# Graph network, third layer: messages written in place, scores made ahead from broadcast keys, block ends spread out, three edge counts to a word

## The chip, the cores and the metric

The kernel runs on one core of a Trainium2 chip. The metric is the device time of one execution in microseconds (us), the median of several runs. Its engines are TensorE (PE in the profile; PEld is its weight load), VectorE (DVE), ScalarE (ACT), GpSimd (POOL) and SyncE (SP). Each works through its own list of instructions in order. SP issues plain transfers, POOL the indirect ones that gather rows by index; both are carried out by 16 DMA engines.

## The reference

Four graph layers work in turn on 6250 nodes of 256 features and 100000 edges sorted by target; each adds its result to `x` and normalises. The change is in the third, two graph-attention passes, and in a table that the fourth uses:

```python
# third layer, one pass (two are made, each followed by gelu); edges and one self loop per node
h = (h_in @ W).reshape(n, 4, 64)
alpha_s = jnp.sum(h * a_s, axis=-1); alpha_d = jnp.sum(h * a_d, axis=-1)
e = leaky_relu(alpha_s[src] + alpha_d[dst], 0.2)
ex = exp(e - m[dst])                       # m: maximum over a target's edges
alpha = ex / segment_sum(ex, dst)[dst]
out = segment_sum(h[src] * alpha[:, :, None], dst) + b
# fourth layer
msg_sum = segment_sum(x[src], dst); mean = msg_sum / max(count, 1)
sage = mean @ W_l.T + b_l + x @ W_r.T
out = relu(relu(sage) @ W_ln.T + x)
```

## The kernel before

The nodes are cut into 50 blocks of 125. The edges that lead to a block lie in 16 chunks of 128 (and two chunks of overflow that 25 blocks share). A piece is four chunks of one block, so a pass over the edges makes 200 pieces. For each pass the table `hs_table` in device memory holds a row of 264 numbers per node: 256 features, four source scores and four target scores.

`piece2` handles one piece. It gathers the 4 x 128 source rows into a tile `g` (four indirect transfers on POOL, one per chunk; `gather`, L932) and makes one-hot matrices `st` from the target keys (DVE, `one_hots`, L941). To give each edge its target's score, PE transposes the one-hots (L2085), ACT copies them as bf16 into `ts` (L2088), and PE multiplies them with the block's target scores, kept as three bf16 parts `ad_parts` (L2093, twelve products into `pe`). DVE adds source and target scores (`e`, L2049) and applies the leaky relu (`r`, L2043); ACT takes exponentials twice, into a small strip of PSUM (`weights_p`, which shares a PSUM tile with the constant `iota_p` and goes by that name in the profile, L2052) and into the last column of the message tile (L2053). DVE multiplies features and weights into the message tile `msg` (L2055). PE sums the messages by target with the one-hots into `ps` (L2127; f32 products appear twice each). Self loops enter through a tile `own`, loaded by SP, its messages `mine`, and a product with the identity (L2120). After a block's last piece, `finish2` divides by the summed weights, adds the bias, takes gelu (L2002 to L2011), and either makes the next pass's table row (first pass) or normalises `x` and writes two tables for the fourth layer (second pass).

The order on PE, DVE and ACT is written out by hand. A piece is a generator that yields group names. `Turns` calls, once a turn, the groups in a fixed order; a plain name means "in the next turn", a "+" in front "later in this turn". A turn starts one new piece, so about six pieces are under way: new, transposes, copy and score products, `e`, product, sum. The order on POOL and SP follows the order in which their instructions are made. POOL is ahead of the others as far as free `g` tiles (nine) allow.

Beside the pieces, in most turns, `count_edges` makes one step of another job: for the first 24 blocks of targets it counts the edges from each source to each target, into `a_table` (bytes). For a source block and a range of four target blocks (500 columns), DVE makes one-hots `a_hot` per chunk (L1965), PE sums them by source (L1975), ACT writes bytes and checks the sum (L1951). There are six ranges, in which 3, 5, 4, 7, 8 and 6 chunks can hold edges: 33 per source block.

Of the kernel before, what the change touches and what calls it, by code (L numbers as in the profile page):

```python
# [17 lines left out]
P = 128  # L18
# [638 lines left out]
def gnn_stack_kernel(ctx: ExitStack, tc: tile.TileContext, ins, out):  # L657
# [55 lines left out]
    ND, RB = 24, 4  # L713
    RW, NR = RB * B, ND // RB
    assert ND % (2 * RB) == 0 and ND < NB and RW <= 512 and NB % 2 == 0
    reach = []
    for r in range(NR):
        e0, e1 = (E * k * RW / N for k in (r, r + 1))
        g0, g1 = (
            int((e + side * 5.5 * (e * (1 - e / E)) ** 0.5) // (GQ * EQ)) for e, side in ((e0, -1), (e1, 1))  # L720
        )
        c0 = max(0, int(place_of(g0 * GQ * EQ, -1)) // P) if g0 else 0
        reach.append((c0, min(CM, int(place_of((g1 + 1) * GQ * EQ, 1)) // P + 1)))
    DC = max(c1 for c0, c1 in reach)
    COUNT_STEPS = NB * NR
# [16 lines left out]
    with ExitStack() as fast:  # L742
# [8 lines left out]
        nc.gpsimd.iota(pidx, pattern=[[1, 1]], base=0, channel_multiplier=1, allow_small_or_imprecise_dtypes=True)  # L751
        ident = const.tile([P, P], F32, name="ident")
# [37 lines left out]
        xr_table = dram.tile([N, D], F32, name="xr_table_f")  # L790

# [210 lines left out]
        def by_target(pool, psum):  # L1002
# [76 lines left out]
            yield  # L1079
            p_row = psum.tile([1, NB + 1], F32, name="p_row")  # L1080
# [504 lines left out]
        class Turns:  # L1585
# [7 lines left out]
            def step(self, item):  # L1593
                group = next(item[0], None)
                if group is None:
                    self.items.remove(item)
                elif group[0] == "+":
                    item[1:] = group[1:], self.now
                else:
                    item[1:] = group, self.now + 1  # L1600
# [8 lines left out]
        def run_pass(turns, makers, beside=None):  # L1609

            for t, make in enumerate(makers):
                turns.add(make())
                turns.turn()
                if t >= len(makers) - 10:
                    turns.turn()
                if beside:
                    beside(t)
# [141 lines left out]
        def features(work, bank, a, w, b, table):  # L1759
# [11 lines left out]
            yield "+fin"  # L1771
            ad, r = hs[:, D + 4 :], work.tile([B, 4], F32, name="ad_r")
# [158 lines left out]

        def count_edges():


            nodes = ap.tile([P, RB, B], F16, name="a_nodes", bufs=1)
            nc.vector.scalar_tensor_tensor(
                nodes, iota[:, :RB, None].to_broadcast([P, RB, B]), float(B),
                iota_p[:, None, :B].to_broadcast([P, RB, B]), op0=ALU.mult, op1=ALU.add,
            )
            nodes = nodes.rearrange("p b n -> p (b n)")  # L1940
            ends = ap.tile([P, NB, DC], F32, name="a_ends", bufs=1)
            nc.vector.tensor_copy(ends, idx_s[:, :, :DC])
            most = max(c1 - c0 for c0, c1 in reach)
            steps = [(s, r) for s in range(NB) for r in range(NR)]
            sts, rows, accs, hots = {}, {}, {}, {}
            for k in range(len(steps) + 2):
                if k >= 2:
                    s, r = steps[k - 2]
                    if r == 0:
                        rows[s] = ap.tile([B, ND * B], U8, name="a_row")  # L1950
                    nc.scalar.activation(  # L1951
                        rows[s][:, r * RW : (r + 1) * RW], accs.pop((s, r))[:B], AF.Copy,
                        accum_out=counted[:B, s * NR + r : s * NR + r + 1],
                    )
                    if r == NR - 1:
                        move(nc.sync, a_table[s * B : (s + 1) * B, :], rows.pop(s))
                        del sts[s]
                if k < len(steps):
                    s, r = steps[k]
                    c0, c1 = reach[r]  # L1960
                    if s not in sts:
                        sts[s] = one_hots(ap, key_s[:, s, :DC], DC, DC, 2, F16, "a_st")
                    hots[k] = ap.tile([P, most, RW], F16, name="a_hot", bufs=2)
                    for i, c in enumerate(range(c0, c1)):
                        nc.vector.tensor_scalar(  # L1965
                            hots[k][:, i, :], nodes, ends[:, s, c : c + 1], float(-r * RW), op0=ALU.subtract,
                            op1=ALU.is_equal,
                        )
                if 0 <= k - 1 < len(steps):
                    s, r = steps[k - 1]  # L1970
                    c0, c1 = reach[r]
                    hot = hots.pop(k - 1)
                    accs[s, r] = apsum.tile([P, 512], F32, name="a_acc")[:, :RW]
                    for i, c in enumerate(range(c0, c1)):
                        nc.tensor.matmul(  # L1975
                            accs[s, r], sts[s][:, c, :], hot[:, i, :], start=(c == c0), stop=(c == c1 - 1)
                        )
                yield

        counted = ap.tile([P, NB * NR], F32, name="counted", bufs=1)  # L1980
        nc.vector.memset(counted, 0.0)
        counting = count_edges()


        for layer in range(2):
            table = hs_tables[layer]
            with tc.tile_pool(name=f"f2{layer}", bufs=1) as pool, tc.tile_pool(
                name=f"f2w{layer}", bufs=2
            ) as work, tc.tile_pool(name=f"f2g{layer}", bufs=9) as gp, tc.tile_pool(
# [6 lines left out]
                turns = Turns(("act", "e", "msg", "fin", "ps", "late", "pe", "tp", "new"))  # L1996

                def finish2(b):
                    whole = sums.pop(b)
                    ps = whole[:B, : D + H2].rearrange("p (h c) -> p h c", h=H2)  # L2000
                    rden = rdens[:B, b, 4 * layer : 4 * layer + 4, None]
                    nc.vector.tensor_scalar(rden, ps[:, :, C2:], 1e-30, None, op0=ALU.max)  # L2002
# [3 lines left out]
                        a.rearrange("p (h c) -> p h c", h=H2), ps[:, :, :C2], rden.to_broadcast([B, H2, C2])  # L2006
                    )
                    nc.vector.tensor_add(a, a, bias[:B, :])
                    yield "act"
                    gl = work.tile([B, D], F32, name="gl")  # L2010
                    nc.scalar.activation(gl, a, AF.Gelu)  # L2011
                    if layer == 0:
                        yield "+late"
                        yield from features(work, lambda: whole, gl, w_gat, b, hs_tables[1])
                    else:
                        yield "+fin"
                        nc.vector.tensor_add(x_sb[:, b, :], x_sb[:, b, :], gl)
                        norm(work, b, False)
                        yield "act"
                        xp = work.tile([B, 3, D], BF16, name="xp")  # L2020
                        nc.scalar.copy(xp[:, 0, :], x_sb[:, b, :])
                        yield "+fin"
                        x_r = work.tile([B, D], F32, name="x_r")
                        nc.vector.tensor_sub(x_r, x_sb[:, b, :], xp[:, 0, :])
                        yield "+late"
                        pt = turned(whole, x_sb[:, b, :])
                        yield "act"
                        nc.scalar.copy(xp[:, 1, :], x_r)
                        xT = kept(work, pt, "xT")
                        yield "+fin"  # L2030
                        nc.vector.tensor_sub(xp[:, 2, :], x_r, xp[:, 1, :])
                        move(nc.sync, block_rows(x_table, b), xp.rearrange("p k d -> p (k d)"))
                        yield "+late"
                        product(whole[:B, :D], [(xT, w_r)])
                        yield "act"
# [4 lines left out]
                def weights(e, n, parts):  # L2040

                    r = work.tile([P, 4, H2], F32, name=f"r{parts}")[:parts, :n, :]
                    nc.vector.scalar_tensor_tensor(r, e, 0.2, e, op0=ALU.mult, op1=ALU.max)  # L2043
                    return r.rearrange("p n h -> p (n h)")

                def messages(g, n, ad, msg, k):

                    e = work.tile([P, 4, H2], F32, name="e")
                    nc.vector.tensor_add(e[:, :n, :], g[:, :n, D : D + 4], ad)  # L2049
                    r = weights(e[:, :n, :], n, P)  # L2050
                    pp = weights_p[:, 4 * H2 * k : 4 * H2 * (k + 1)]
                    nc.scalar.activation(pp[:, : n * H2], r, AF.Exp)  # L2052
                    nc.scalar.activation(msg[:, : n * H2, C2], r, AF.Exp)  # L2053
                    yield "msg"
                    nc.vector.tensor_mul(  # L2055
                        msg[:, : n * H2, :C2].rearrange("p (n h) c -> p n h c", h=H2),
                        g[:, :n, :D].rearrange("p n (h c) -> p n h c", h=H2),
# [304 lines left out]
```

## Time and profile before

| what | value |
|---|---|
| median of 3 runs (lowest, highest) | 5450.11 us (5446.99, 5450.46) |
| the profiled execution | 6347.38 us |
| its span, first to last instruction | 6345.5 us |
| mean granted clock of PE in it | 0.876 |
| first pass of the third layer, first to last L2055 | 2844.3 to 4133.4 us |
| second pass | 4197.4 to 5560.4 us |
| gathers of the two passes (L932, hs_table) | 1600, mean 951 ns |

The profile shows a single execution, which is longer than the runs without it. Busy times can't be added across engines, since they overlap. A row of waits reads: engine and line that waited, "<-" what released it, total us, times, longest. In a row of a group, the part after "|" gives busy us and the mean ns of one instruction, then the idle time of the engine before it.

### The profile page before, as it was taken

What the parts mean: (1) busy time and instruction counts of PE and PEld (TensorE: products, weight loads), DVE (VectorE), ACT (ScalarE), POOL (GpSimd) and SP (SyncE); (2) the same over time, 40 slices, a digit from 0 to 9 for tenths busy, and PEclk for the clock granted to TensorE, in tenths of its full rate; (3) what the DMA queues carried; (4) which work ended last, traced back from release to release, by engine and by line L of the source; (5) the groups of instructions that cost most, each with busy time, mean ns of one, the idle gap of its engine ahead of it and who ended that gap; (6) DMA issues with size and microseconds to landing.
All of it is one profiled execution on the core that took longest, in us unless ns stands there. A gap on an engine that the chain in (4) does not pass through costs nothing.

```text
span 6345.5 us, 85961 instructions
## 1 busy us (share of the span) xinstructions
PE 4651.2 (73%) x28778; PEld 3328.7 (52%) x28778; DVE 3995.7 (63%) x11239; ACT 2312.8 (36%) x6308; POOL 3590.8 (57%) x3709
## 2 busy tenths in 40 slices
PE   1567888867777777757777777747766776779996
PEld 0445666645555555535555555535545555545554
DVE  7786666646777777746666666646767767623233
ACT  4016677932322222213333333323333333323332
POOL 5776666645555555535555555455555555455554
PEclk9778999988999999978888888878888878889997
DMA  5555555545655556533333333333333333377774
GB/s 152 152 163 157 160 157 151 153 129 170 177 173 171 172 167 174 171 86 96 105 102 102 102 101 101 90 83 102 104 100 104 105 102 97 93 189 206 205 193 122
DMA packets 383758, 862.39 MB, mean 136 GB/s; under 512 B 85018, under 2 KB 208376, under 8 KB 383304
## 3 DMA queue, kind: packets, MB, share of 16 engines
q0 software_dynamic: 221184, 670.83, 39.0%
q1 hardware_dynamic: 162120, 185.97, 10.2%
q8 instruction: 228, 3.74, 0.2%
q14 instruction: 226, 1.85, 0.1%
HBM read 769.69 MB, written 86.78 MB: 135 GB/s over the span
## 4 chain that ended last, share of the span: by engine, by line
PE 35%; DVE 22%; issue 13%; another core or an unknown queue 10%; ACT 9%; POOL 5%; DMA 3%; SPq 0%; DVEq 0%; ACTq 0%; POOLq 0%
PE ps L2127 6%; PE d L2274 6%; POOL g L932 5%; PE ps L985 5%; PE a_acc L1975 4%; DVE msg L2055 3%; PE po L928 2%; DVE s L1821 2%; PE tp L2085 2%; DVE msg L1828 2%; PE acc L1519 2%; DVE a_hot L1965 2%; DMA g<-kv_table_f,idx_s 2%; PE pt L928 2%
## 5 line engine op out<-in xcount | busy, mean ns | idle before, releaser
L932 POOL DMA_INDIRECT g<-hs_table_f,idx_d x1600 | 1520.9, 951 | 1249.8 <-DVE msg L2055 493.8
L932 POOL DMA_INDIRECT g<-kv_table_f,idx_s x784 | 746.7, 952 | 548.9 <-issue 204.2
L932 POOL DMA_INDIRECT g<-h_table_f,idx_d x800 | 799.5, 999 | 430.6 <-issue 213.8
L2127 PE MATMUL ps<-msg,st 128*125 128x260 f32 x3200 | 919.6, 434 | 97.2 <-DVE msg L2055 52.9
L2127 PEld LDWEIGHTS ps<-msg,st 128*125 128x125 f32 x3200 | 688.5, 218 | 291.6 <-issue 82.8
L1975 PE MATMUL a_acc<-a_hot,a_st 128*128 128x500 f16 x1650 | 497.6, 444 | 373.6 <-ACT a_row L1951 282.8
L2055 DVE TENSOR_TENSOR msg<-g,iota_p 128x1024 f32<-128x1024 f32 x400 | 488.2, 1221 | 403.6 <-ACT iota_p L2052 328.0
L932 POOL DMA_INDIRECT g<-x_table_f,idx_d x416 | 395.7, 951 | 383.4 <-PE ps L985 191.4
L985 PE MATMUL ps<-g,st 128*128 128x256 bf16 (+1 forms) x3648 | 519.3, 293 | 126.1 <-issue 60.4
L985 PEld LDWEIGHTS <-st 128*128 128x128 bf16 x4104 | 419.2, 104 | 255.8 <-issue 150.3
L2088 ACT CAST ts<-tp 125x512 bf16<-125x512 f32 x400 | 233.3, 583 | 820.7 <-remote 479.2
L1965 DVE TENSOR_SCALAR a_hot<-a_nodes,a_ends 128x500 f16<-128x500 f16 x1650 | 505.2, 372 | 18.1 <-remote 18.1
L1908 PE MATMUL ps<-msg,st 128*125 128x264 f32 x1600 | 437.7, 419 | 100.6 <-DVE msg L1828 73.3
L1975 PEld LDWEIGHTS <-a_st 128*128 128x128 f16 x1650 | 180.5, 109 | 577.1 <-issue 484.6
L1908 PEld LDWEIGHTS ps<-msg,st 128*125 128x125 f32 x1600 | 301.4, 199 | 237.3 <-DVE msg L1828 103.9
L941 DVE TENSOR_TENSOR st<-iota_p,key_d 128x500 f32<-128x500 f32 (+1 forms) x550 | 409.8, 746 | 20.8 <-ACT iota_p L2052 16.3
L2274 PE MATMUL d<-cnt,xs 125*128 125x500 bf16 x1800 | 401.2, 378 | 16.9 <-issue 16.5
L1889 DVE TENSOR_TENSOR prod<-g,qe 128x512 f32<-128x512 f32 x400 | 262.3, 684 | 197.5 <-PE qe L1882 68.3
L2049 DVE TENSOR_TENSOR e<-g,pe 128x16 f32<-128x16 f32 x400 | 65.1, 163 | 454.7 <-remote 352.1
L1882 PE MATMUL qe<-q,ts 125*128 125x256 bf16 x2400 | 318.9, 286 | 29.0 <-DVE prod L1889 24.2
L2085 PE MATMUL tp<-ident,st 128*125 128x128 f32 x1600 | 308.5, 314 | 40.6 <-issue 30.1
L1532 ACT ACTIVATE oa<-t_f,blk 125x128 f16<-125x128 f16 x800 | 310.7, 388 | 74.4 <-remote 48.1
(453 smaller groups left out, 8768.0 us busy)
## 6 DMA issues: line engine op xcount, KB each, us to landing
g<-hs_table_f,idx_d POOLq DMA_INDIRECT x1600
xs<-x_table_f SPq DMA_DIRECT2D x75, 336.0 KB
a_table_f<-a_row SPq DMA_DIRECT2D x50, 328.1 KB
few<-a_table_f SPq DMA_DIRECT2D x75, 218.8 KB
g<-h_table_f,idx_d POOLq DMA_INDIRECT x800
g<-kv_table_f,idx_s POOLq DMA_INDIRECT x784
hs_table_f<-hs SPq DMA_DIRECT2D x100, 115.5 KB
own<-hs_table_f SPq DMA_DIRECT2D x100, 115.5 KB
```

What stands on the lines that cost most here:

```text
L932: nc.gpsimd.indirect_dma_start(out=g, out_offset=None, in_=table, in_offset=bass.IndirectOffsetOnAxis(ap=idx, axis=0))
L941: nc.vector.tensor_tensor(st, iota_p[:, None, :w].to_broadcast([P, n, w]), key[:, :, None].to_broadcast([P, n, w]), op=ALU.is_equal,)
L985: nc.tensor.matmul(ps[:, :m], st[:, i, :], g[:, i, k * D : k * D + m], start=(c0 + i == 0 and k == 2), stop=(c0 + i == CH - 1 and k == 0),)
L1532: nc.scalar.activation(oa[:, i, :], o1[:, i, :], AF.Copy, scale=val_a[:, at])
L1882: nc.tensor.matmul(qe[:, i, :], ts[:, i0 + i, :], q[:, k * D : (k + 1) * D], start=(k == 0), stop=(k == 2))
L1908: nc.tensor.matmul(sums[b][:B, : D + H1], hot, m[:, i * H1 : (i + 1) * H1, :].rearrange("p h c -> p (h c)"), start=(c == 0), stop=(c == CH ...
L1965: nc.vector.tensor_scalar(hots[k][:, i, :], nodes, ends[:, s, c : c + 1], float(-r * RW), op0=ALU.subtract, op1=ALU.is_equal,)
L1975: nc.tensor.matmul(accs[s, r], sts[s][:, c, :], hot[:, i, :], start=(c == c0), stop=(c == c1 - 1))
L2055: nc.vector.tensor_mul(msg[:, : n * H2, :C2].rearrange("p (n h) c -> p n h c", h=H2), g[:, :n, :D].rearrange("p n (h c) -> p n h c", h=H2) ...
L2085: nc.tensor.transpose(tp[:, i, :], st[:, i, :], ident)
L2127: nc.tensor.matmul(sums[b][:B, : D + H2], hot, m[:, i * H2 : (i + 1) * H2, :].rearrange("p h c -> p (h c)"), start=False, stop=(c == CH - 1),)
L2274: nc.tensor.matmul(accs[h][q], xs[:, i, j * D + h * P : j * D + (h + 1) * P], cnt[:, i, q * RW : (q + 1) * RW], start=(s + i == 0 and j == 2),
```

## The change

1. *Scores from broadcast keys.* At the start, the keys of every block (an edge's place among the block's nodes) are written to device memory as bf16 rows (`keys_d`). `keys2` loads a block's row into all 125 partitions, so partition p can compare all 2048 keys with p: ACT computes (key - p) squared and then relu(1 - that), in place, four chunks at a time (`node_hots`). That gives the transposed one-hots of a whole block; PE multiplies them with `ad_parts` and ACT copies the 16 x 4 scores to `ends_d`. A pass starts with eight turns of keys alone (`LEAD_K`), and keys are begun eight turns ahead of their block's first piece. The per-piece transposes, `ts` and the per-piece `pe` go.
2. *In place.* The weights go into columns 256 to 259 of `g` (over the source scores), and the product into its feature columns; `own` is treated in the same way. PE sums from `g`. There is no `msg` or `mine` tile. `g` has 11 tiles instead of 9. The one-hots for the sum are made in the turn of the product.
3. *Block ends.* `Turns` takes a number ahead of a name ("3act": three turns later). A block's end moves from PE to ACT or DVE with one to three turns between. Four PSUM banks for sums instead of three; the groups have another order.
4. *Counts.* Three ranges of 500 columns share one accumulation: an edge adds 1, 256 or 65536 to the column, by its range. `less` and `unit` are made once for all chunks. Each source block has two such words, of 5 and 9 possible chunks, in steps of at most three: 14 instead of 33. ACT copies a word to int32 and then writes its low three bytes as three rows of counts.

The core of the diff:

```diff
+        keys_d = dram.tile([NB, CAP], BF16, name="keys_d_f")
...
+            k_rows = pool.tile([NB, CAP], BF16, name="k_rows")
+            nc.scalar.copy(k_rows, k_f)
+            nc.sync.dma_start(out=keys_d, in_=k_rows)
...
-                    item[1:] = group, self.now + 1
+                    name = group.lstrip("0123456789")
+                    item[1:] = name, self.now + int(group[: len(group) - len(name)] or 1)
...
+        LEAD_K = 8
+        def run_pass(turns, makers, beside=None, keys=None):
+            per = len(makers) // NB
+            for t in range(-LEAD_K if keys else 0, 0):
+                if (t + LEAD_K) % per == 0:
+                    turns.add(keys((t + LEAD_K) // per))
+                turns.turn()
             for t, make in enumerate(makers):
+                if keys and (t + LEAD_K) % per == 0 and (t + LEAD_K) // per < NB:
+                    turns.add(keys((t + LEAD_K) // per))
...
-                    hots[k] = ap.tile([P, most, RW], F16, name="a_hot", bufs=2)
-                    for i, c in enumerate(range(c0, c1)):
+                    hots[k] = ap.tile([P, 3, RW], BF16, name="a_hot", bufs=4)
+                    for i in reversed(range(n)):
                         nc.vector.tensor_scalar(
-                            hots[k][:, i, :], nodes, ends[:, s, c : c + 1], float(-r * RW), op0=ALU.subtract,
-                            op1=ALU.is_equal,
+                            hots[k][:, i, :], column, less[:, s, c0 + i : c0 + i + 1],
+                            unit[w][:, s, c0 + i : c0 + i + 1], op0=ALU.is_equal, op1=ALU.mult,
                         )
...
+                    word = ap.tile([B, RW], I32, name="a_word")
+                    nc.scalar.copy(word, accs.pop((s, w))[:B])
                     nc.scalar.activation(
-                        rows[s][:, r * RW : (r + 1) * RW], accs.pop((s, r))[:B], AF.Copy,
+                        rows[s][:, w * WORD * RW : (w + 1) * WORD * RW].rearrange("p (q j) -> p q j", q=WORD),
+                        word.bitcast(U8).rearrange("p (j q) -> p q j", q=4)[:, :WORD, :], AF.Copy,
...
+        G_BUFS, ST_BUFS = 11, 9
+        def node_hots(kb, q):
+            part = kb[:, q * 4 * P : (q + 1) * 4 * P]
+            nc.scalar.activation(part, part, AF.Square, bias=minus[:B])
+            nc.scalar.activation(part, part, AF.Relu, bias=ones[:B, 0:1], scale=-1.0)
...
-                turns = Turns(("act", "e", "msg", "fin", "ps", "late", "pe", "tp", "new"))
+                turns = Turns(("late", "keys", "pe", "keys2", "pe2", "e", "msg", "ps", "fin", "new", "act"))
...
+                def steps_of(g, n, ad, k, p=P):
+                    e = work.tile([P, 4, H2], F32, name="e")[:p, :n, :]
+                    nc.vector.tensor_add(e, g[:, :n, D : D + 4], ad)
+                    r = work.tile([P, 4, H2], F32, name="r")[:p, :n, :]
+                    nc.vector.scalar_tensor_tensor(r, e, 0.2, e, op0=ALU.mult, op1=ALU.max)
+                    pp = weights_p[:p, 4 * H2 * k : 4 * H2 * k + n * H2].rearrange("p (n h) -> p n h", h=H2)
+                    nc.scalar.activation(pp, r, AF.Exp)
+                    nc.scalar.activation(g[:, :n, D : D + H2], r, AF.Exp)
+                    yield "msg"
+                    feats = g[:, :n, :D].rearrange("p n (h c) -> p n h c", h=H2)
+                    nc.vector.tensor_mul(feats, feats, pp[:, :, :, None].to_broadcast([p, n, H2, C2]))
...
+                def keys2(b):
+                    kb = work.tile([B, CAP], BF16, name="kb")
+                    move(nc.sync, kb, keys_d[b : b + 1, :].to_broadcast([B, CAP]))
+                    yield "2keys"
+                    ts = kb.rearrange("p (c e) -> p c e", e=P)
+                    pe = psum.tile([P, CM, H2], F32, name="pe")
+                    for q in range(CM // 4):
+                        node_hots(kb, q)
+                        yield "+pe2" if q % 2 else "+pe"
+                        for c in range(4 * q, 4 * q + 4):
+                            for k in range(3):
+                                nc.tensor.matmul(
+                                    pe[:, c, :], ts[:, c, :], ad_parts[:, b, k, :], start=(k == 0), stop=(k == 2)
+                                )
+                        if q % 2:
+                            yield "keys"
+                        else:
+                            yield "+keys2"
+                    yield "act"
+                    ends_d[b] = work.tile([P, CM, H2], F32, name="ends_d", bufs=3)
+                    nc.scalar.copy(ends_d[b], pe)
...
-                    yield "tp"
-                    tp = psum.tile([B, 4, P], F32, name="tp", bufs=2)
-                    for i in range(n):
-                        nc.tensor.transpose(tp[:, i, :], st[:, i, :], ident)
-                    yield "act"
-                    ts = work.tile([B, 4, P], BF16, name="ts", bufs=3)
-                    nc.scalar.copy(ts[:, :n, :], tp[:, :n, :])
-                    yield "pe"
...
+                    yield "2e"
+                    steps = steps_of(g, n, ends_d[b][:, c0 : c0 + n, :], (c0 // 4) % 2)
...
+                    st = one_hots(work, key_d[:, b, c0 : c0 + n], n, 4, ST_BUFS)
...
-                        yield "fin"
+                        yield "3fin"
                         yield from finish2(b)
```

## The prediction

> **What bounds the kernel now.** I read the page's busy shares first, then one row per stage of the third layer, then who waits for whom in it. Each of the layer's two passes makes 200 turns of one piece (50 blocks of four pieces), and each turn has one wide message product on VectorE (L2055), so the pass is measured from the first of these to the last.
>
> ```profile
> span 6345.5 us, 85961 instructions
> PE 4651.2 (73%) x28778; PEld 3328.7 (52%) x28778; DVE 3995.7 (63%) x11239; ACT 2312.8 (36%) x6308; POOL 3590.8 (57%) x3709
> ```
> ```profile
> core 0: us, PE busy (x) PEld busy (x) DVE busy (x) ACT busy (x) POOL busy (x), PEclk, DMA share, GB/s
> 2844.00:4133.00 1289.00, 1001.43 (x6207) 722.84 (x6208) 839.23 (x2294) 439.99 (x1214) 730.65 (x770) 0.86 0.37 99
> 4197.00:5560.00 1363.00, 952.16 (x6052) 700.67 (x6052) 935.11 (x2670) 490.37 (x1306) 730.42 (x768) 0.83 0.36 99
> ```
>
> No engine is full. Per turn the first pass takes 1289/200 = 6.45 us and the second 6.82. Of this PE is busy 5.0 and 4.8, DVE 4.2 and 4.7, ACT 2.2 and 2.5. GpSimd shows 3.65 us, but one gather is 0.95 us and the next starts 0.30 later even with nothing to wait for:
>
> ```profile
> 4381.49 0.95 POOL L932 DMA_INDIRECT g<-hs_table_f,idx_d  x1 [0.30 <-issue]
> 4382.75 0.95 POOL L932 DMA_INDIRECT g<-hs_table_f,idx_d  x1 [0.30 <-issue]
> ```
>
> So four gathers need 4 x 1.25 = 5.0 us: the floor of a turn. What lies above it is waiting in a ring, as the waits of the second pass (GpSimd, VectorE) and of the first (ScalarE) show:
>
> ```profile
> POOL g L932 <- DVE msg L2055: 279.9, 106, 8.6
> POOL g L932 <- DVE rdens L2002: 104.2, 31, 4.6
> ...
> DVE e L2049 <- remote: 151.6, 41, 9.0
> DVE msg L2055 <- ACT iota_p L2052: 150.5, 126, 4.2
> DVE e L2049 <- PE pe L2093: 35.7, 28, 3.1
> ...
> ACT ts L2088 <- remote: 260.1, 45, 13.0
> ACT ts L2088 <- PE pe L2093: 103.5, 21, 7.5
> ACT ts L2088 <- PE tp L2085: 69.5, 32, 8.2
> ```
>
> GpSimd waits for the product that frees a gather tile; VectorE waits at the score sum `e` for PE; ScalarE waits at the copy `ts` for PE's transposes. "Remote" is a release without a recorded releaser: there the semaphore that `e` and `ts` wait for is PE's. The ring is one-hots (DVE), transposes (PE), `ts` (ACT), `pe` (PE), `e` (DVE), exponentials (ACT), product (DVE).
>
> **The base of the sum.** The profiled execution took 6347.38 us (span 6345.5), the runs 5450.11: 0.859 of it. I assume that ratio for the passes: 5.53 and 5.86 us a turn in the timed runs. I do not scale the 1.25 us of a gather, since nothing around it waits; that choice is the largest uncertainty here.
>
> **The change part by part.**
>
> *Scores from broadcast keys.* Out go, per turn, four transposes and one `ts` copy (0.586 us of ACT, L2088). The PE rows at full clock, start to start:
>
> ```profile
> 4373.87 0.45 PE L2093 MATMUL pe<-ad_parts,ts 125*128 125x4 bf16 x12
> 4374.18 0.68 PE L2085 MATMUL tp<-ident,st 128*125 128x128 f32 x4
> 4374.69 1.86 PE L1975 MATMUL a_acc<-a_hot,a_st 128*128 128x500 f16 x8
> 4376.39 0.60 PE L2120 MATMUL ps<-mine,ident 125*125 125x260 f32 x2
> ```
>
> Transposes take 0.51 us a turn, the 12 `pe` products 0.31 (they stay, 24 at a time in two of four turns), one count product 1.70/8 = 0.21. In come per block: eight ACT operations on 125x512 bf16 (nearest row L2088; its source is PSUM in f32, ends 0.45 to 0.65; I take 0.57) = 4.6 us against 4 x 0.586 = 2.3 before, a 128x64 copy (about 0.2) and one more exponential of the block's own rows (0.2): ACT +2.7 a block, 0.7 a turn, so 3.2 of 5.0. A key load of 2 x 125 x 2048 = 512 KB a block joins SP's queue: 99 GB/s at a share of 0.37 is about 268 GB/s in all, so 1.9 us on free engines, 3 on these; it is issued two turns (10 us) before use. On SP it stands behind the write of `xp`, which waits for VectorE; that write belongs to a block whose turn came earlier, so it delays keys by less than those two turns. What this buys: `e` now waits only for its gather and for scores copied five turns before. The PE waits at `e` (151.6 + 35.7) and all waits at `ts` go; where they go is GpSimd, which becomes the engine behind which everything stands.
>
> *In place.* The product writes into `g`: the same 1024 f32 elements, 1.22 us, no change. The tile is now held until PE has summed it, turn 4 after the gather, instead of the product in turn 5; 11 tiles instead of 9. The next gather can start 7 turns (35 us) ahead, against 4 before. So GpSimd should wait for none of the tiles.
>
> *Block ends three turns a hop.* The same instructions, about 5 us of DVE a block. In the steady part nothing waits for them: a sum's bank is held 15 turns of 16 (four banks). Two more blocks are unfinished when a pass ends: 2 x 5 = 10 us a pass, hidden by nothing. At its start eight turns hold keys alone: 16 x 0.57 = 9 us of ACT beside the first gathers (5 us, plus the table's last write), so I add 8. Both passes: 36.
>
> *Counts.* Products and `a_hot` fall from 33 to 14 a source block, 1650 to 700. PE saves 950 x 0.21 = 200 us, 0.5 a turn. An `a_hot` now takes two scalars from memory. The rows for that are the norm's (two pointers, 273 ns) and its first step (constants, 154):
>
> ```profile
> L1965 DVE TENSOR_SCALAR a_hot<-a_nodes,a_ends x1650: 329/341/590, 2802.1 to 5505.9; 128x500 f16<-128x500 f16 x184
> L864 DVE TENSOR_SCALAR ln_t<-ln_y,ln_w x300: 272/273/275, 1518.1 to 5569.1; 125x1 f32<-125x1 f32 x150
> ```
>
> So 341 + 119 = 460 ns; bounds 341 and, at one element a step, about 700. DVE goes from 4.1 x 0.34 = 1.4 to 1.75 x 0.46 = 0.8 a turn: -0.6 (at 700: -0.2). The byte copy of ACT is three times as wide but a third as frequent: even. The set-up (some 28 operations at 0.4 to 0.7, 15 us of DVE) lies under the 44 gathers (55 us) that fill the 11 tiles.
>
> Sum per turn: GpSimd 5.0; DVE 3.6 and 4.1; PE 5.0 and 4.8 less 1.0, about 3.9; ACT about 3.1. GpSimd is the bound with a margin of 0.9. With the shared gathers and 2% of jitter I take 5.1.
>
> *The clock.* The Trainium skill ("TensorE: Matmul & The Clock Gate", "HAM oscillation") speaks against all this: the array falls to half clock after an idle window of about 3.4 us, and PE loses a fifth of its work. At full clock the new turn has 38/4 summing products of 0.22 (2.1 us), 0.3 of `pe`, 0.37 of counts and 0.3 of block ends: 3.1 us. By the rule at its worst (half clock throughout) it is 6.2 us and PE is the bound: 400 x (6.2 - 5.7) + 36, about 5690. By the rows (0.86 and 0.83) it is 3.7. I take the rows: with sums in every turn, no idle stretch need reach 3.4 us of a 5 us turn.
>
> Timed: 200 x (5.53 - 5.1) + 200 x (5.86 - 5.1) = 238 saved, less 36: 202, so 5450 - 202 = 5248, I say 5250. In a profiled execution, where waits look longer (5.4 a turn): 200 x (6.45 + 6.82 - 10.8) - 36 = 458, about 5890.
>
> **The rivals.** Two runs can differ by about 0.2% here, so less than that counts as no change.
> - *The gather is quicker when nothing is recorded* (0.859 x 1.25 = 1.07 us): the floor falls to 4.3, the turn to about 4.6: 200 x (0.93 + 1.26) - 36 = 402, 5050. For it: everything else is quicker by 14%. Against: its duration never varies.
> - *The timed turn is already near 5.3*, since the PE waits are what recording stretches: 400 x 0.2 - 36 = 44, 5405; at 5.2 nothing is left and it is no change. For it: several releases by PE come 5 to 20 us after the product's recorded end.
> - *Slower: ACT takes PE's place in the ring.* In two of four turns it does four key operations (2.3 us) and a table load (1.28) before the exponentials, which the next product needs, with the sums on PE and the release of `g` behind it. At worst 3.6 us twice a block; it decides from 1.2 us a heavy turn, where 2.4 a block cancels the gain (4 x 0.6). At half the worst: 100 x (3.6 - 2.4) + 36, 5610. For it: VectorE waits 150.5 us there already. Against: ACT would be at 3.2 of 5.0 us and the product comes a turn later.
> - *The change doesn't do what it says*: the counts and scores are simply fewer instructions, so this could only be through order, which is the rival above.
>
> **How the numbers follow.** Likeliest case 0.45 (5200 to 5330 alone); quicker gather 0.20; small gain 0.20, of which 0.04 is within 0.2%; slower, by ACT or by the clock, 0.15. The range cuts 0.15 above and less than 0.05 below: 5040 to 5440. Faster 0.81, same 0.04, slower 0.15.
>
> **What the profile will show.** Right: GpSimd gathers 1.25 us apart through both passes with few waits for VectorE or PE, turns of 5.0 to 5.5 us, no wait of `e` for PE, `a_hot` near 460 ns x700, key operations near 570 ns. Wrong if: VectorE waits at the product for ACT for more than 1 us a turn, PE's clock is under 0.7, `a_hot` is above 700 ns, or the stretches between the passes grow by much more than 18 us each.

## The result: 0.9% slower, and the profile after

The changed kernel takes 5494.74 us (median of four runs, 5492.74 to 5500.70) against 5448.55 us before (5446.97 to 5450.46): a ratio of 1.0086, 95% interval 1.0069 to 1.0104. A second measurement gave 1.0096 (1.0077 to 1.0116). The forecast was 5250 us.

The first lines of the page after:

```profile
span 5490.9 us, 82002 instructions
## 1 busy us (share of the span) xinstructions
PE 4175.7 (76%) x26228; PEld 3030.0 (55%) x26228; DVE 3750.4 (68%) x10315; ACT 2684.5 (49%) x6609; POOL 3588.3 (65%) x3710
```

This profiled execution agrees with the timed runs and is one of them (5492.74 us); that of the kernel before (6347 us) had not agreed. So the kernel before was profiled a second time, on the chip of the first experiments. The page of this second execution:

```profile
span 5442.1 us, 85961 instructions
```

> The kernel before, unchanged, profiled once more. Theory A (the first profiled execution was stretched by late releases from PE, and an execution that is not stretched has turns of about 5.3 us): the span is near 5450 us, with the second layer's wide products lasting about 1185 us instead of 1326, as in the changed kernel's profile, and the two passes of the third layer about 1060 and 1060 us from first to last product. Theory B (recording always costs this kernel 16%, by its transposes and small products): the span is again near 6350 us.

It took 5443.88 us. Its span is that of the timed runs, and even the second layer, which the change doesn't touch, is shorter than in the first profile: 1188 us instead of 1326 from its first wide product to its last (1184 in the changed kernel). So recording does not by itself lengthen an execution. Later experiments ran on a chip on which the kernel before took 6434 us in the median of seven timed runs, at a mean granted clock of 0.87 instead of 0.93. The forecast had read one long execution (6347 us) and set it against runs of the short kind. What makes an execution long was not found.

From here on "before" is the second execution. The expectation had the total right, but not the split into passes of 1060 us each. The two passes of the third layer, one row each, from first to last wide product (columns: length, busy us and instructions of each engine, PE's granted clock, share of the DMA engines, GB/s). Before:

```profile
core 0: us, PE busy (x) PEld busy (x) DVE busy (x) ACT busy (x) POOL busy (x), PEclk, DMA share, GB/s
2507.00:3513.00 1006.00, 881.76 (x6224) 664.54 (x6223) 838.87 (x2296) 438.86 (x1214) 758.96 (x795) 0.96 0.47 130
3544.00:4709.00 1165.00, 902.92 (x6065) 680.40 (x6062) 932.81 (x2671) 494.49 (x1306) 756.78 (x794) 0.87 0.43 119
```

After:

```profile
2517.00:3546.00 1029.00, 786.50 (x4817) 575.31 (x4814) 708.51 (x1793) 613.92 (x1323) 748.69 (x788) 0.83 0.54 149
3586.00:4765.00 1179.00, 821.63 (x4763) 606.92 (x4760) 823.67 (x2267) 660.77 (x1451) 752.47 (x789) 0.80 0.50 137
```

A turn took 5.03 us in the first pass before and 5.82 in the second; after, 5.15 and 5.90. Four gathers of 1.25 us make 5.0: the first pass had stood at that floor already. VectorE is busy 3.5 and 4.1 us a turn, as forecast (3.6 and 4.1). PE stands at 3.9 and 4.1 us (forecast 3.9), but it came from 4.4 and 4.5 us and not from 5.0 and 4.8. ScalarE rose by 40% and 34%. The 48.8 us between the two spans lie here: first pass +23.6, second +14.7, the stretch before the first pass +14.5 (36.4 to 50.9), that between the passes +8.7 (31.3 to 40.0), everything else -12.7.

Who waits in the second pass, before (total us, times, longest):

```profile
ACT x_sb L898 <- DVE m L897: 210.7, 49, 4.7
PE a_acc L1975 <- ACT a_row L1951: 209.4, 48, 6.6
...
POOL g L932 <- DVE msg L2055: 143.3, 88, 3.2
DVE msg L2055 <- ACT iota_p L2052: 132.6, 155, 2.3
```

And after:

```profile
DVE g L2113 <- ACT iota_p L2109: 307.2, 192, 5.5
ACT x_sb L902 <- DVE m L901: 252.9, 48, 5.4
...
PE pe L2136 <- ACT kb L2034: 210.6, 126, 6.4
...
POOL g L936 <- PE ps L2182: 110.1, 57, 5.4
```

The waits of `e` for PE are gone, as forecast, but before they had been only 52 us of the second pass. VectorE's product now waits for the exponentials in nearly every turn (192 of 200), 307 us instead of 133. One such turn, first on ScalarE, then on VectorE, then on PE (start, length, instruction; in brackets the idle time before it and what ended that; `...` marks lines left out):

```profile
4001.28 0.19 ACT L2109 ACTIVATE iota_p<-r 128x16 f32<-128x16 f32 x1 [0.50 <-DVE r L2107]
...
4001.68 0.18 ACT L2109 ACTIVATE iota_p<-r 125x4 f32<-125x4 f32 x1
...
4005.60 0.56 ACT L1989 CAST a_word<-a_acc 125x500 int32<-125x500 f32 x1
4006.19 1.45 ACT L1990 ACTIVATE a_row<-a_word 125x1500 uint8<-125x1500 uint8 x1
...
4007.64 0.71 ACT L2033 ACTIVATE kb<-kb,minus 125x512 bf16<-125x512 bf16 x1
...
4009.74 0.72 ACT L2034 ACTIVATE kb<-kb,ones 125x512 bf16<-125x512 bf16 x1
4010.48 1.28 ACT L2109 ACT_TABLE_LOAD   x1
4011.78 0.19 ACT L2109 ACTIVATE iota_p<-r 128x16 f32<-128x16 f32 x1
```
```profile
4006.33 0.17 DVE L2107 SCALAR_TENSOR_TENSOR r<-e 128x16 f32<-128x16 f32 x1
4012.00 1.22 DVE L2113 TENSOR_TENSOR g<-g,iota_p 128x1024 f32<-128x1024 f32 x1 [5.49 <-ACT iota_p L2109]
4013.14 0.41 DVE L2113 TENSOR_TENSOR own<-own,iota_p 125x256 f32<-125x256 f32 x1
...
4017.26 0.16 DVE L901 SCALAR_TENSOR_TENSOR m<-mv,r 125x1 f32<-125x1 f32 x1
```
```profile
4019.08 1.19 PE L932 MATMUL ps<-w_r,xT 128*125 128x256 f32 x2 [2.95 <-ACT xT L924]
```

The leaky relu `r` of the newest piece is ready at 4006.5, and its exponentials run at 4011.8, after the byte copy of the counts, four key operations and a table load. VectorE stands still for 5.49 us until then, with the product next in its list. But this product belongs to the piece before. The product of the block's own rows (`own`, 4013.14) comes with it, so its exponentials are those at 4001.28 and 4001.68, which were done 10 us earlier.

This is the rule and not an exception. Matched in their order, 190 of the 200 products of the second pass begin only when the exponentials of the *next* piece are done, while their own had been done for 5.5 us in the median. In the kernel before it is 190 as well; there the next piece's exponentials came sooner. The product needs no value of the next piece. What they share is the PSUM tile of `weights_p`, in which each piece has its own strip, and the next piece's exponentials stand ahead of the product in the program. The likely reason is therefore that the order is kept for the whole tile. No run gave the strips tiles of their own, so this is not shown.

Behind that product in VectorE's list stands the norm of a block's end (until 4017.4), for which ScalarE waits 5.35 us; behind ScalarE's part of the norm stands its copy `xT`; for that PE waits 2.95 us. GpSimd issues a gather every 1.25 us in this stretch, but over the pass it waits 110 us for sums that free a tile: the ring is now longer than its 5.0 us.

### The profile page after: what moved, and what is told of

Read it like the earlier page. It is cut to its first block, busy times and chain, and to the rows that moved or that the text cites. A ratio compares the mean times of both kernels' runs of the same rounds, so it can differ in the third digit from the quotient of the medians.

```text
span 5490.9 us, 82002 instructions
## 1 busy us (share of the span) xinstructions
PE 4175.7 (76%) x26228; PEld 3030.0 (55%) x26228; DVE 3750.4 (68%) x10315; ACT 2684.5 (49%) x6609; POOL 3588.3 (65%) x3710
## 4 chain that ended last, share of the span: by engine, by line
DVE 29%; PE 21%; POOL 14%; ACT 14%; issue 13%; DMA 8%; ACTq 0%; SPq 0%; DVEq 0%; POOLq 0%
POOL g L936 14%; PE d L2328 7%; DVE g L2113 3%; DVE st L945 3%; DMA g<-hs_table_f,idx_d 3%; PE ps L989 3%; ACT kb L2033 2%; DMA g<-kv_table_f,idx_s 2%; DVE s L1842 2%; PE ps L2182 2%; DVE msg L1849 2%; DMA g<-h_table_f,idx_d 2%; PE qe L1903 2%; ACT kb L2034 2%; DVE prod L1910 2%
## 5 line engine op out<-in xcount | busy, mean ns | idle before, releaser
L2182 PE MATMUL ps<-g,st 128*125 128x260 f32 x3200 | 943.4, 448 | 26.3 <-issue 23.1
L2113 DVE TENSOR_TENSOR g<-g,iota_p 128x1024 f32<-128x1024 f32 x400 | 488.5, 1221 | 592.2 <-ACT iota_p L2109 590.2
L2182 PEld LDWEIGHTS ps<-g,st 128*125 128x125 f32 x3200 | 714.9, 227 | 198.7 <-issue 33.0
L2136 PE MATMUL pe<-ad_parts,kb 125*128 125x4 bf16 x4800 | 180.9, 166 | 375.0 <-ACT kb L2034 363.1
L2136 PEld LDWEIGHTS <-kb 125*128 125x128 bf16 x4800 | 156.1, 100 | 454.9 <-ACT kb L2034 441.7
L1929 PEld LDWEIGHTS ps<-msg,st 128*125 128x125 f32 x1600 | 290.8, 192 | 162.9 <-DVE msg L1849 68.9
L902 ACT ACTIVATE x_sb<-x_sb,m,r 125x256 f32<-125x256 f32 x150 | 90.0, 600 | 564.4 <-DVE m L901 564.4
L1540 ACT ACTIVATE ob<-t_f,s_f 125x128 bf16<-125x128 f16 x800 | 311.7, 390 | 0.0
L2034 ACT ACTIVATE kb<-kb,ones 125x512 bf16<-125x512 bf16 x400 | 288.6, 721 | 13.0
L2033 ACT ACTIVATE kb<-kb,minus 125x512 bf16<-125x512 bf16 x400 | 284.5, 711 | 17.4 <-DMA kb<-keys_d_f 17.4
```

The source lines that it names most:

```text
L1929: nc.tensor.matmul(sums[b][:B, : D + H1], hot, m[:, i * H1 : (i + 1) * H1, :].rearrange("p h c -> p (h c)"), start=(c == 0), stop=(c == CH ...
L2033: nc.scalar.activation(part, part, AF.Square, bias=minus[:B])
L2034: nc.scalar.activation(part, part, AF.Relu, bias=ones[:B, 0:1], scale=-1.0)
L2113: nc.vector.tensor_mul(feats, feats, pp[:, :, :, None].to_broadcast([p, n, H2, C2]))
L2136: nc.tensor.matmul(pe[:, c, :], ts[:, c, :], ad_parts[:, b, k, :], start=(k == 0), stop=(k == 2))
L2182: nc.tensor.matmul(sums[b][:B, : D + H2], hot, m[:, i, : D + H2], start=False, stop=(c == CM - 1))
```

## The experiments

**Take the keys off ScalarE.** VectorE compares in one step:

```diff
-            nc.scalar.activation(part, part, AF.Square, bias=minus[:B])
-            nc.scalar.activation(part, part, AF.Relu, bias=ones[:B, 0:1], scale=-1.0)
+            nc.vector.tensor_scalar(part, part, pidx[:B], None, op0=ALU.is_equal)
```

> The changed kernel with the keys compared on VectorE (one is_equal per quarter of a block instead of two ScalarE operations of 0.71 us). Theory A (ScalarE is in the ring of the second pass: the key operations stand ahead of the exponentials that the next product needs): ScalarE loses 5.7 us a block, VectorE gains about 4 x 0.3 = 1.2; the second pass falls from 5.9 us a turn to about 5.3, the first stays at 5.15: 5494 - 200 x 0.6 = about 5375. Rival (VectorE and its own chain of block ends bound the second pass): VectorE's added 1.2 us a block make it slower by up to 60 us: 5550. Rival (GpSimd bounds both passes): no change, 5495.

5378.3 us, 0.9875 (0.9858 to 0.9891) of the kernel before. The comparison takes 0.346 us where two operations of 0.71 and 0.72 stood. The rows of the two passes:

```profile
2516.00:3508.00 992.00, 752.38 (x4826) 550.23 (x4823) 768.50 (x1980) 369.60 (x951) 749.35 (x785) 0.86 0.56 154
3542.00:4648.00 1106.00, 784.16 (x4750) 584.17 (x4751) 876.83 (x2455) 417.19 (x1079) 758.64 (x792) 0.82 0.53 146
```

ScalarE's work falls by 244 us in each pass, VectorE's rises by 60 and 53, and the passes are 37 and 73 us shorter. The total was as expected (5375), the split was not: the first pass was to stay and the second to give 120 us. The first is back at the gathers' floor. It can be a little below 1000 us, since some gathers lie ahead of its first product.

**The same instructions, another order.** The key operations go behind the exponentials and the sums of their turn:

```diff
-Turns(("late", "keys", "pe", "keys2", "pe2", "e", "msg", "ps", "fin", "new", "act"))
+Turns(("late", "e", "msg", "ps", "keys", "pe", "keys2", "pe2", "fin", "new", "act"))
```

> The changed kernel with the key operations moved behind the exponentials and the sums within a turn, the same instructions. Theory A: the product no longer waits for ScalarE behind 2.8 us of key operations, so most of its wait of 291 us in the second pass goes: about 5400. Rival (ScalarE is simply too full, wherever the keys stand, since it waits in order for the norm and then for the sums): the wait moves, within 20 us of 5494.

5353.5 us, 0.983 (0.9813 to 0.9846). No work was taken away, ScalarE is as busy as in the changed kernel (620 and 670 us in the passes), and 141 us go. So the fault is the place, not the amount. In the second pass, now 1076 us, the product's wait and ScalarE's for the norm are shorter:

```profile
DVE g L2113 <- ACT iota_p L2109: 202.6, 193, 3.5
...
PE pe L2136 <- ACT kb L2034: 149.0, 132, 5.2
...
ACT x_sb L902 <- DVE m L901: 126.9, 48, 4.4
...
POOL g L936 <- PE ps L2182: 40.8, 37, 4.9
```

The order changed on PE as well: the key products, which wait for ScalarE, now stand behind the sums that free the gather tiles, and GpSimd's wait for these sums falls from 110 to 41 us. The run does not tell apart what the place on ScalarE and the place on PE are worth.

**Make the suspect dearer.** A third operation per quarter:

```diff
             nc.scalar.activation(part, part, AF.Relu, bias=ones[:B, 0:1], scale=-1.0)
+            nc.scalar.copy(part, part)
```

> The changed kernel with a third ScalarE operation per quarter of a block (a copy in place, 0.7 us), 2.8 us more a block. Theory A: the second pass has no slack on ScalarE, so it takes most of it: 50 x 2.8 = 140 us, the first pass some of it (its ScalarE is on the edge): 5494 + 140 to 250, about 5680. Rival (GpSimd or VectorE bound): under 30 us more.

5712.54 us, 1.0488 (1.0471 to 1.0506). The copy takes 0.617 us, 400 of them 247; the kernel is 218 us longer than the changed one, 95 in the first pass, 105 in the second and most of the rest in the stretches before them. So nearly nine tenths of ScalarE's added time appears in the kernel's.

**Both cures together**, keys on VectorE and behind the exponentials:

> Keys on VectorE and behind the exponentials and sums. If both cures take away the same wait (ScalarE's key operations ahead of the exponentials): no better than the better of the two, 5350 to 5380, since VectorE carries 1.2 us a block more. If they take away different waits: about 5290.

5385.93 us, 0.9892 (0.9875 to 0.9908): no better than the keys on VectorE alone and worse than the order alone. That fits two cures for one wait: the product's is 178 us in the second pass with the keys on VectorE, 203 in the new order and 184 with both.

**One hop of the block's end.** On the exponentials-first order, `xT` is copied a turn earlier:

```diff
-                        yield "2act"
+                        yield "act"
                         xT = kept(work, pt, "xT")
-                        yield "late"
+                        yield "2late"
```

> The exponentials-first order of run three, with the copy of xT one turn after the transposes instead of two and the product with it two turns after the copy (the bank of the sum is held as long as before). Theory: PE no longer stands at the head of a turn for ScalarE's copy at the tail of the one before (149 us of waits at L932 in the second pass there), and the sums behind it come earlier: second pass 1076 to about 1040, 5353 to about 5320. Rival (PE has slack, so its wait there costs nothing): 5353.

5353.14 us, 0.9834 (0.9818 to 0.9851), as without it; the rival was right. PE's wait for `xT` (149 us in the second pass) goes, but its waits for keys rise from 149 to 188 us and 60 us for the norm are new. PE waits elsewhere, and the second pass stays at 1077 us.

**The counts alone.** The kernel before, with the counts of the change. For want of room it has one accumulator bank and three `a_hot` tiles where the changed kernel has two and four, and reads a word one step earlier:

```diff
-                    nc.scalar.activation(
-                        rows[s][:, r * RW : (r + 1) * RW], accs.pop((s, r))[:B], AF.Copy,
...
+                    word = ap.tile([B, RW], I32, name="a_word")
+                    nc.scalar.copy(word, accs.pop((s, w))[:B])
...
-                            hots[k][:, i, :], nodes, ends[:, s, c : c + 1], float(-r * RW), op0=ALU.subtract,
-                            op1=ALU.is_equal,
+                            hots[k][:, i, :], column, less[:, s, c0 + i : c0 + i + 1],
+                            unit[w][:, s, c0 + i : c0 + i + 1], op0=ALU.is_equal, op1=ALU.mult,
```

> The kernel before with the counts of the change alone (three ranges to a word; one accumulator bank and three a_hot tiles for want of room, the word read one step earlier). Theory A (the first pass before was at the gathers' 5.03 us a turn, the second bound by the order of VectorE, PE and ScalarE at 5.82): the first pass stays at about 1005 us, the second gives up part of the 0.5 us a turn that VectorE and PE lose: 1165 to about 1100; about 5380. Rival (the counts fill idle time in both passes): no change, 5445.

5309.77 us, 0.9752 (0.9736 to 0.9768); again with others below, 5315.02, 0.9763 (0.9745 to 0.9782). This beats the kernel before by 2.4% and the changed one by 3.3%. The rows of its passes, and PE's wait at the count products in the second:

```profile
2521.00:3513.00 992.00, 814.23 (x5716) 623.53 (x5713) 713.71 (x1786) 457.92 (x1050) 749.83 (x787) 0.94 0.47 131
3544.00:4591.00 1047.00, 819.26 (x5648) 642.86 (x5645) 820.91 (x2259) 501.89 (x1175) 760.27 (x794) 0.89 0.48 132
```
```profile
PE a_acc L1993 <- ACT a_word L1969: 77.5, 18, 6.4
```

The first pass was at the floor and gains 13 us; the second gains 118. There PE had waited 209 us at the count products for ScalarE to empty the one accumulator; a third as many words leave 77.5 us of such waits. VectorE's work falls too, by 112 us, and no run separates the two. The stretch before the first pass is 9.5 us longer; what is new in it is the set-up of `less` and `unit` on VectorE.

**All but the counts.** The changed kernel with `count_edges`, its step list and its accumulator as before:

> The changed kernel with the counts of before (33 products a source block). Theory A (scores from keys cost ScalarE time in the ring, and the counts' saving had covered part of it): slower than the changed kernel by the counts' share, 60 to 120 us: 5550 to 5610. Rival (VectorE and PE have slack while ScalarE is the bound): within 20 us of 5494.

5605.58 us, 1.0298 (1.0281 to 1.0316): 161 us slower than the kernel before, 95 of it in the first pass. So the change holds a gain of about 134 us and a loss of about 161. Their sum, +27, is not quite the measured +46 (+53 the second time): together the two cost some 20 us more than one by one. Which part of them does stays open.

**In place alone, and the hops undone.** The counts with the gathered messages in place and 11 tiles, but the old scores, order and block ends:

```diff
-                    nc.scalar.activation(msg[:, : n * H2, C2], r, AF.Exp)
+                    nc.scalar.activation(g[:, :n, D : D + H2], r.rearrange("p (n h) -> p n h", h=H2), AF.Exp)
```

and the changed kernel with `"3fin"`, `"3act"` and `"2act"` written as `"fin"` and `"act"`:

> Counts of the change and messages in place with 11 gather tiles, on the old chain of scores (transposes, ts, per-piece pe), the old order of groups and the old block ends. Theory (in place costs nothing by itself and the loss of the change is the keys' ScalarE time in front of the exponentials): as counts alone, 5310, or up to 30 better by the two more tiles. Rival (holding the gather tile until PE has summed it delays the gathers): 5340 or more.

> The changed kernel with block ends one turn a hop again (3 and 2 turns become 1), all else as changed. Theory (the hops took waits between PE and ScalarE away and only lengthen the drains): slower than 5494 in the second pass by some tens of us, the stretch between the passes shorter by up to 9 us: about 5510. Rival (the hops are part of the loss): 5450 to 5480.

These two ran on the chip that takes 6434.26 us for the kernel before. There they took 6217.25 (0.9665, 0.9643 to 0.9687) and 6264.32 us (0.974, 0.972 to 0.9761). They were run again on another chip, beside the changed kernel and the counts alone:

> The changed kernel once more, beside the three below. If this chip runs the kernel before in about 5445 us: 1.009 of it, as measured. If it runs it in about 6430 us, as the last one did, where PE's releases come late: the forecast made from such an execution should hold there, 0.92 to 0.96 of the kernel before.

> Ends one turn a hop, as in run ten, beside the changed kernel on the same chip. Theory (the three-turn hops keep PE and ScalarE from waiting for each other): slower than the changed kernel by 20 to 60 us. Rival: faster by 15 to 45.

> Counts and in place, as in run nine, beside counts alone. Theory: equal to counts alone or up to 30 us better. Rival (the tile is held until PE has summed it, so gathers come later): 20 us or more worse.

> Counts alone once more, on the chip of the three above: 0.975 of the kernel before on a chip that runs that in 5445 us, about 0.96 on one that runs it in 6430 us (fewer PE releases to be late).

With the kernel before at 5443.69 us: changed 5496.69, hops undone 5540.85 (1.0177, 1.0157 to 1.0197), in place 5321.62 (0.9772, 0.9752 to 0.9792), counts alone 5315.02. Writing in place, with its two more tiles, neither gains nor costs (6.6 us, inside the intervals).

The long hops are worth 44 us in all, but in opposite ways in the two passes. First the changed kernel, its two passes and the product's wait in the first:

```profile
2521.00:3551.00 1030.00, 778.70 (x4824) 571.12 (x4822) 708.60 (x1793) 614.30 (x1325) 749.82 (x789) 0.84 0.54 149
3588.00:4768.00 1180.00, 821.18 (x4764) 606.10 (x4765) 823.44 (x2268) 660.98 (x1456) 753.80 (x789) 0.80 0.50 137
DVE g L2113 <- ACT iota_p L2109: 283.6, 194, 6.1
```

Then the same with one-turn hops, followed by its waits in the second pass:

```profile
2521.00:3517.00 996.00, 761.03 (x4828) 564.28 (x4828) 715.99 (x1798) 614.60 (x1329) 752.14 (x789) 0.85 0.56 154
3556.00:4814.00 1258.00, 808.23 (x4756) 579.36 (x4757) 825.40 (x2267) 657.98 (x1455) 755.19 (x789) 0.77 0.46 128
DVE g L2113 <- ACT iota_p L2109: 163.9, 192, 3.1
```
```profile
DVE g L2113 <- ACT iota_p L2109: 382.5, 193, 4.6
...
PE ps L919 <- ACT x_sb L902: 215.5, 49, 9.3
```

Without the long hops the second pass is 78 us longer, and PE stands 215 us for ScalarE's norm at the next block's end. The first pass is 34 us *shorter* and back at the gathers' floor. So the total came as expected, but in the first pass the rival was right: there the hops are part of the loss. The stretches ahead of the passes hardly differ (51 and 40 us instead of 51 and 37).

Taken together: the first pass returns to about 1000 us by any of three ways (keys on VectorE, keys behind, one-turn hops), the second is helped only by the two that move the keys. Most of the loss is thus the scores from keys in the order in which they were put. The other new places in the order and the fourth bank were not tried alone. And even in the better order the scores from keys gain nothing here: 5353.5 us, against 5309.77 with the counts alone.

The kernel with one-turn hops is 2.6% faster than the kernel before on one chip and 1.8% slower on another. On the chip of the 6434 us the waits named "remote" are there again: with the old chain of scores 139 us at `e` and 179 at `ts` in the first pass of the in-place kernel. Scores made ahead don't wait for those, and the two passes of the kernel with one-turn hops are 42 us shorter than those of the in-place kernel there. But the stretches ahead of its passes are 87 us longer, for a reason not found, so in all it is 47 us longer. The changed kernel itself was not run on that chip.

## Why the prediction was wrong, point by point

The forecast was a gain of 202 us and the result a loss of 46. By the two profiles: the first pass was to become 86 us shorter and became 24 longer, the second was to become 152 shorter and became 15 longer; 36 us more were allowed for the stretches, and 23 came.

- *The base of the sum* failed first. "I assume that ratio for the passes: 5.53 and 5.86 us a turn" took one long execution as an even stretch of the short ones. Undisturbed, the second pass is 5.82, as assumed, but the first is 5.03, 0.03 over the gathers' floor. The 86 us forecast for it weren't there. Nor was most of what the scores from keys were to remove: the waits of `e` for PE in the second pass, 151.6 + 35.7 us in the long execution, are 52 us in the short one. The floor itself (1.25 us a gather, not scaled) was right, on both kinds of chip.
- *The slower rival was the case*, at 0.15. The step that failed is the one that put it aside: "the product comes a turn later", so that four key operations and a table load ahead of the exponentials were put at nothing. The product does come a turn later than its own exponentials, but it waits for those of the next piece, which are in its own turn. The rival's break-even was 1.2 us a heavy turn; the product's wait rose from 133 to 307 us in the second pass, 1.7 us for each of its 100 heavy turns, and the two cures gave 116 and 141 us in all. The sum per turn treated engines as if only their totals mattered: ScalarE's 3.3 us a turn in the second pass (3.1 forecast) fits easily in 5.0, and it was in the ring all the same. The sign that the forecast named for being wrong came, more than 1 us a turn of this wait: 1.5.
- *Sizes.* A key operation takes 0.71 to 0.72 us, above the upper end of 0.65 given; the nearest row had its source in PSUM and another operation. At 800 of them this is 115 us more of ScalarE than forecast. `a_hot` takes 405 ns instead of 460:

```profile
L2003 DVE TENSOR_SCALAR a_hot<-a_column,a_less,a_unit x700: 392/405/633, 2515.2 to 4740.9; 128x500 bf16<-128x500 f16 x175
```

- *Counts* were mis-placed in the sum. They were put down as slack on VectorE and PE under the gathers; in the second pass, which was not at the floor, they are worth 118 us. The byte copy "even" was right in amount (0.56 + 1.45 + 0.19 us for each of 100 words, 0.57 + 0.19 for each of 300). But its 1.45 us comes in one piece and can stand ahead of the exponentials, as in the turn above; what that costs was not tried.
- *The stretches.* The set-up was said to be hidden under the gathers that fill the tiles. It costs 9.5 us: the first of those gathers waits for a block end on VectorE, and the set-up is interleaved with that block end. What is left of the longer stretches, 5 and 9 us, goes with the eight turns of keys.
- *In place* cost nothing, as said. GpSimd "should wait for none of the tiles" held nearly in the first pass (22 us), not in the second (110 us).
- *The hops* were said to cost nothing in the steady part and 10 us at the end of a pass. They cost 34 us in the first pass and earn 78 in the second, and without them the stretches are no shorter.
- *The clock.* PE's granted clock fell from 0.96 to 0.83 and from 0.87 to 0.80, and PE's busy time in the first pass by 11% for 23% fewer products. That PE came out near the 3.9 us forecast is luck: too high a base less too large a saving. The rule of the Trainium skill ("TensorE: Matmul & The Clock Gate", "HAM oscillation"), that idle stretches over about 3.4 us halve the clock, was set aside in the forecast; the clock moved in its direction, though far from its worst, and how long PE's idle stretches were was not measured. That PE is not the bound is seen from the exponentials-first order, whose first pass is 997 us at a clock of 0.84.

## What to carry to other kernels

Before a forecast, hold the profiled execution against the timed runs: if it is 16% longer, its waits are those of another situation and its ratio is no scale for a single stage; look for a stage whose floor is known (here the gathers) and ask what it would be undisturbed. When engines work through hand-written lists, totals per turn say what could be reached, not what is: for each wait in the ring, count what stands ahead of the releasing instruction in its own engine's list. Find out, too, which piece that instruction belongs to: a consumer placed a turn behind its own producer may still be waiting for a newer one. Work made ahead of need belongs behind the instruction that others wait for; moving the key work (eight operations on ScalarE a block, and the products that follow) behind the exponentials and sums was worth 2.6% here without removing any of it.

## What the runs showed of the hardware that was not expected

- The same kernel took 5444 to 5446 us on three chips and 6434 on a fourth. A gather every 1.25 us was the same on both kinds; on the fourth, waits of up to 28 us for PE ended without a recorded releaser.
- A `tensor_scalar` on 128x500 with two scalars from memory took 405 ns, against 341 with one from memory and one constant. The operations and the output's type differ as well, so the 64 ns are not shown to be the second scalar's price.
- ScalarE's Square and Relu on bf16 in SBUF took 0.71 us for 512 elements, a plain copy of the same tile 0.617, and a copy from PSUM with a cast 0.586.
